# Turning narrow heads' probabilities in quarters of 32 rows, and what was rearranged to make room for it

## The chip, the cores and the metric

The kernel runs on one core of a Trainium2 chip. The metric is the device time of one execution in microseconds (us). The engines are named as in the profile: PE is TensorE's matmul stream and PEld its weight loads, DVE is VectorE, ACT ScalarE, POOL GpSimd, SP the engine that issues most DMAs. The profile also gives the clock that TensorE was granted, as a share of full speed.

## The reference, cut to what matters

Four transformer layers run one after the other over x of 16 items, 256 tokens and 128 features, in float32. Each layer is an attention part and a feed-forward part, both on a layernorm of x and both added to x. All four attentions have 16 heads; in layers 0 and 2 a head is 64 wide, in layers 1 and 3 it is 8 wide.

```python
for item in range(16):
    # layer 0: q, k normalized per head, two null keys, causal, distance bias slope[h] * -|i - j|
    # layer 1: q from a latent of 64, one k and v shared by all 16 heads of 8, causal
    # layer 2: qkv with bias, all tokens see all;   layer 3: 16 heads of 8, causal within 128 tokens
    p = softmax(q @ k.T * scale + bias_or_mask)        # per head, 256 x 256 (258 in layer 0)
    x[item] += concat_heads(p @ v) @ w_out (+ b_out)
    # feed-forward: gelu MLP (0); gated ternary MLP, two 512x512 gelu layers (1);
    # one of 8 experts per token (2); gated mix with the token before (3)
```

## The kernel before

The kernel doesn't issue its instructions in the order of its source. It describes the work as *steps*, and a planner (`Plan`, L68 to L228) decides in which order the steps of each engine are written. A step names its engine (`"AD"` is ACT or DVE, whichever is free), a rank `p`, a cost in ns, the values that it reads, writes or modifies, and, for PE, a *mode*: steps of one mode use the array in the same shape of tiles ("T" is the whole array, "S" row groups of 64, "S4" row groups of 32, "O" and "O4" column groups of 64 and 32). `Plan.run` goes through its own model of time, keeps PE in one mode while it can, and charges `SWITCH` (130 ns in its model) for a change. On the chip every engine then follows the written order, with semaphores between the engines.

Values live in *homes*, pools of equal tiles. The home "t" is the eight PSUM banks of 512 columns; a bank is taken when the first step that touches it is written and given back when the last one is. "pT" holds transposed probabilities (six tiles of 512 columns), "probs" the probabilities before that, "Q", "K" and "V" the inputs of the wide heads, "r" 512-column scratch.

**Narrow heads (layers 1 and 3, `narrow_unit`, L544).** An item has three units. A unit has sixteen blocks of 128 x 128 probabilities. Its scores are four matmul groups in row groups of 32, into four banks (mode "S4"). DVE adds the mask and takes the minimum (L563), ACT takes exponentials (L569), and then PE turns the blocks (L581): four steps in mode "T", each with four whole blocks into one bank, and each followed by a copy by ACT (L383) or DVE (L385) into one "pT" tile. The products (mode "O4", column groups of 32) need all four tiles and add up into one bank `o` per item.

**Wide heads (layers 0 and 2, `wide_unit`, L445).** An item has four units of four heads. Their blocks are turned in two halves of 64 rows (L491): the halves use two row groups of the array and two banks, in mode "S", the same as their scores.

**Layer 0 before its units (`prep0`, L716).** `project` makes q and k for the two halves of the tokens (n is 0 to 3, c is 0 or 1) and sums squares per head; POOL takes the power -1/2 (`rsqrt`, L371); `scaled` multiplies (DVE, L751), turns four whole blocks (L756, mode "T") and copies the bank into "Q" or "K". The distance bias is a table `bias` of 16 x 258 columns, one row per head, which DVE makes at the start (L676) and the reduction at L792 adds. The table shares its memory with the weights of layer 1's feed-forward, which are loaded when layer 0 is over (`to_w1`, L873).

**Layer 2 before its units (`prep2`, L1035).** The bias of v is added by DVE as v leaves PSUM (L1063), from a tile `bv` that holds it in all partitions.

**The start.** SP issues the loads of x and weights, then the load of `bv`, then two DMAs that fill the experts' row buffers with zeros (L312), in pieces of 32 elements.

Of the kernel before, what the change touches and what calls it, by code (L numbers as in the profile page):

```python
# [15 lines left out]
P = 128  # L16
# [9 lines left out]
    ("a2bq", 8), ("a2bk", 8),  # L26
# [205 lines left out]
def preln_d4_kernel(ctx: ExitStack, tc: tile.TileContext, x_in, vecs, rows, bv2, nullk, nullv,  # L232
# [50 lines left out]
    bv = cp.tile([P, 1024], F32, tag="bv", name="bv")  # L283
    nc.sync.dma_start(out=bv, in_=bv2.broadcast_to([P, 1024]))
# [22 lines left out]
    zero = cp.tile([P, D // 4], F32, tag="zero", name="zero")  # L307
    nc.gpsimd.memset(zero, 0.0)
    for part, n in enumerate(EX_BLOCKS):
        ex_rows.append(dp.tile([n * P, D], F32, tag=f"rows{part}", name=f"ex_rows{part}"))  # L310
        ex_y.append(dp.tile([n * P, D], F32, tag=f"y{part}", name=f"ex_y{part}"))
        nc.sync.dma_start(out=ex_rows[part].rearrange("(p j) (s d) -> p (j s) d", p=P, s=4),  # L312
                          in_=zero.unsqueeze(1).broadcast_to([P, 4 * n, D // 4]))
# [43 lines left out]
    plan.home("pT", many(sp, "pT", 6, [512]))  # L357
# [4 lines left out]
    plan.home("small", many(sp, "small", 5, [256]))  # L362
# [3 lines left out]
    def mm(o, lhsT, rhs, start=True, stop=True, **kw):  # L366
        nc.tensor.matmul(o, lhsT, rhs, start=start, stop=stop, **kw)  # L367

# [72 lines left out]
    def bias_x(p, name, b):  # L441
        step("POOL", p, 670, lambda e: nc.gpsimd.tensor_tensor(x_of(b), x_of(b), row_over(name, 2), ALU.add), m=[X[b]])  # L442


    def wide_unit(q, b, u, st, widths, starts, blocks, first, second, kept=None):  # L445
# [3 lines left out]
        banks, pT = [], []  # L449
# [32 lines left out]
        for pair in range(2):  # L482
            t, h = [get("t"), get("t")], [get("pT"), get("pT")]
            pT.append(h)

            def turn(e, pair=pair, t=t):
                for j in range(2):
                    for i, a in enumerate(starts):
                        for z in range(2):
                            r, c = slice(64 * z, 64 * z + 64), j * (w // 2) + i * 64  # L490
                            nc.tensor.transpose(t[z].t[:, c:c + 64], probs[pair].t[r, j, a:a + P], ident[r, r])  # L491

            step("PE", q + 8 + 2 * pair, 120 * len(starts), turn, r=[probs[pair]], w=t, mode="S")
            for z in range(2):
                evac(q + 8 + 2 * pair + z, h[z], t[z], lambda h=h, t=t, z=z: (h[z].t[:, 0:w], t[z].t[:, 0:w]), w)
        o, OT = get("t"), get("OT")

        def products(e):
            for pair in range(2):
                for k, (kc, q0, at) in enumerate(blocks):  # L500
                    for z in range(2):
                        for j in range(2):
# [5 lines left out]
                               pT[pair][z].t[:, a:a + (256 - q0) // 2].rearrange("p (c q) -> p c q", q=64),  # L508
# [3 lines left out]
        step("PE", q + 11.9, 3.36 * cols, products, r=st["V"] + pT[0] + pT[1], w=[o], mode="O")  # L512
# [31 lines left out]
    def narrow_unit(q, b, u, st, mask, mkey):  # L544
# [29 lines left out]
        pT = []  # L574
        for k in range(4):
            t, h = get("t"), get("pT")
            pT.append(h)

            def turn(e, k=k, t=t):
                for g in range(4):  # L580
                    nc.tensor.transpose(t.t[:, g * P:(g + 1) * P], probs[g // 2].t[:, g % 2, k * P:(k + 1) * P], ident)  # L581

            step("PE", q + 8 + k, 436, turn, r=probs, w=[t], mode="T")
            evac(q + 8 + k, h, t, lambda h=h, t=t: (h.t, t.t))
# [4 lines left out]
        def products(e):  # L589
# [3 lines left out]
            for k in range(4):  # L593
                hh, kc = (k, 0) if u == 0 else (2 * u - 2 + k // 2, k % 2)
                a = (256 if hh == 3 else 0) + qc * P
                for g in range(4):
                    mm(o.t[32 * g:32 * g + 32, a:a + P], st["v"](kc, g, hh), pT[k].t[:, g * P:(g + 1) * P],
                       u == 0 and k == 0, u == 2 and k == 3, skip_group_check=True)

        step("PE", q + 11.9, 900, products, r=[st["V"]] + pT, m=[o], mode="O4")  # L600
# [50 lines left out]
    bias_pool = top.enter_context(tc.tile_pool(name="a0c", bufs=1))  # L651
# [8 lines left out]
    A0, A1 = 0, first[1, 0]  # L660
    wqkv = wA[:, w0_at["qkv"]:w0_at["qkv"] + 3072]
# [4 lines left out]
    dist = bias_pool.tile([P, 258], F32, tag="dist", name="dist")  # L666
# [4 lines left out]
    bias = bias_pool.tile([P, NH, 258], F32, tag="bias", name="bias")  # L671
    slope = 2.0 ** (-2.0 ** (-(math.log2(NH) - 3.0)))

    def biases(e, u):
        for h in range(4 * u, 4 * u + 4):
            nc.vector.tensor_scalar(bias[:, h, :], dist, float(slope * slope ** h), None, ALU.mult)  # L676

    for u in range(4):
        step("DVE", 4 * u - 6, 1000, lambda e, u=u: biases(e, u), w=[f"bias{u}"])
# [23 lines left out]
    step("DVE", -13, 100, lambda e: nc.vector.tensor_scalar(nkT.rearrange("p c n -> p (c n)"), nk_ps.t[:, 0:16], kqs, None, ALU.mult),  # L703
# [12 lines left out]
    def prep0(b):  # L716
        st = {}
        lo, hi = A0 + 16 * (b - 1), A0 + 16 * b - 2
        order = ("x p00 p01 p10 p11 p20 p21 t00 p30 t01 p31 t10 v0 t11 v1 v2 t20 v3 t21 t30 t31").split()
# [11 lines left out]
        def project(n, c):  # L731
# [11 lines left out]
            if c == 1:  # L743
                step("DVE", p, 80, lambda e: nc.vector.tensor_scalar(ss[n].t, ss[n].t, 1e-24, None, ALU.max), m=[ss[n]])  # L744
                step("POOL", p - 6, 2892, lambda e: rsqrt(ss[n].t, 16), m=[ss[n]])

        def scaled(n, c):
            i, which = divmod(n, 2)
            p, raw, t = at[f"t{n}{c}"], raws[n, c], get("t")
            r = lambda: raw.t.rearrange("p (h d) -> p h d", d=64)  # L750
            step("DVE", p - 2, 598, lambda e: nc.vector.tensor_tensor(  # L751
                r(), r(), ss[n].t[:, c * 8:(c + 1) * 8].unsqueeze(2).broadcast_to([P, 8, 64]), ALU.mult), r=[ss[n]], m=[raw])

            def turn(e):
                for k in range(4):
                    nc.tensor.transpose(t.t[:, k * P:(k + 1) * P], raw.t[:, k * P:(k + 1) * P], ident)  # L756
# [730 lines left out]
```

## Time and profile before

| | |
|---|---|
| time, median of 3 runs | 2208.14 us (2207.95 to 2212.46) |
| the profiled execution | 2214.85 us |
| its span, from first to last instruction | 2213.1 us |
| mean clock granted to TensorE | 0.99 |
| matmuls and weight loads | 20879 each |
| busy: PE, PEld, DVE, ACT, POOL | 97%, 71%, 75%, 75%, 48% |

The page gives for each engine its busy time, its share of the span and its number of instructions. A busy PE includes the tail of pipelined matmuls, so that successive starts in the timeline say more about speed than durations do. Lines of the timeline give start, duration, engine, source line, operation, what is written and what is read; the shape of the weights stands as rows x columns in use. A float32 matmul appears as two instructions, a transpose as one. By the narrow and wide scores in the timeline, layer 0's units run from about 46 to 628 us, layer 1's from about 650 to 1180, layer 2's from 1158 to 1846 and layer 3's from 1837 to 2188; each layer's feed-forward runs beside the units that follow.

### The profile page before, as it was taken

What the parts mean: (1) busy time and instruction counts of PE and PEld (TensorE: products, weight loads), DVE (VectorE), ACT (ScalarE), POOL (GpSimd) and SP (SyncE); (2) the same over time, 40 slices, a digit from 0 to 9 for tenths busy, and PEclk for the clock granted to TensorE, in tenths of its full rate; (3) what the DMA queues carried; (4) which work ended last, traced back from release to release, by engine and by line L of the source; (5) the groups of instructions that cost most, each with busy time, mean ns of one, the idle gap of its engine ahead of it and who ended that gap; (6) DMA issues with size and microseconds to landing.
All of it is one profiled execution on the core that took longest, in us unless ns stands there. A gap on an engine that the chain in (4) does not pass through costs nothing.

```text
span 2213.1 us, 57690 instructions
## 1 busy us (share of the span) xinstructions
PE 2141.7 (97%) x20879; PEld 1576.0 (71%) x20879; DVE 1657.2 (75%) x6401; ACT 1669.9 (75%) x4735; POOL 1054.0 (48%) x1987
## 2 busy tenths in 40 slices
PE   6999999999999999999999999999999999998997
PEld 3767777777776566665666678888888787786775
DVE  5898888889788575666655557877766788787995
ACT  5988888989889776677756567776666577777995
POOL 6997787878851111111103235554543855226331
PEclk9999999999999999999999999999999999999998
DMA  7000000000020000000000000000432000451000
GB/s 173 2 2 2 2 2 2 2 2 2 2 92 2 1 2 1 1 1 1 1 1 1 1 1 7 7 6 3 120 111 82 26 5 19 133 164 28 12 12 11
DMA packets 58590, 57.78 MB, mean 26 GB/s; under 512 B 27824, under 2 KB 48832, under 8 KB 58304
## 3 DMA queue, kind: packets, MB, share of 16 engines
q1 hardware_dynamic: 55504, 49.06, 7.9%
q0 software_dynamic: 2048, 4.20, 0.6%
q8 instruction: 165, 2.70, 0.5%
q14 instruction: 121, 0.99, 0.1%
q10 hardware_dynamic: 752, 0.83, 0.1%
HBM read 43.85 MB, written 10.22 MB: 24 GB/s over the span
## 4 chain that ended last, share of the span: by engine, by line
PE 78%; DVE 10%; POOL 6%; ACT 3%; issue 2%; DMA 1%; another core or an unknown queue 0%; SPq 0%; POOLq 0%; ACTq 0%; DVEq 0%
PE t5x L367 9%; PE t4x L367 8%; PE t7x L367 8%; PE t2x L367 8%; PE t3x L367 7%; PE t0x L367 7%; PE t1x L367 7%; PE t6x L367 7%; PE t0x L581 1%; PE t1x L581 1%; PE t2x L581 1%; PE t3x L581 1%; PE t5x L581 1%; PE t4x L581 1%; PE t6x L581 1%
## 5 line engine op out<-in xcount | busy, mean ns | idle before, releaser
L442 POOL TENSOR_TENSOR x<-x,row_sb 128x256 f32<-128x256 f32 x48 | 35.0, 728 | 31.9 <-DVE xn1x L411 16.0
L404 POOL TENSOR_SCALAR ln_rs1x<-ln_mv1x 128x2 f32<-128x2 f32 x24 | 4.6, 193 | 76.3 <-DVE ln_mv1x L400 73.4
L991 POOL TENSOR_TENSOR x<-x,sq1x 128x512 f32<-128x512 f32 x4 | 5.1, 1280 | 73.2 <-DVE sq1x L989 73.2
L474 POOL TENSOR_SCALAR probs4x<-probs4x,sums6x 128x256 f32<-128x256 f32 (+2 forms) x40 | 17.6, 457 | 38.5 <-DVE sums6x L469 16.9
L474 POOL TENSOR_SCALAR probs2x<-probs2x,sums6x 128x256 f32<-128x256 f32 (+2 forms) x40 | 17.6, 458 | 37.4 <-DVE sums6x L469 21.5
L474 POOL TENSOR_SCALAR probs2x<-probs2x,sums2x 128x256 f32<-128x256 f32 (+2 forms) x44 | 22.2, 519 | 25.8 <-DVE sums2x L469 25.5
L404 POOL TENSOR_SCALAR ln_rs0x<-ln_mv0x 128x2 f32<-128x2 f32 x21 | 4.0, 193 | 63.2 <-DVE ln_mv0x L400 60.2
L371 POOL TENSOR_TENSOR ss0x<-ss0x,mhalf 128x16 f32<-128x16 f32 x11 | 31.9, 2902 | 2.7 <-DVE ss0x L744 2.6
L371 POOL TENSOR_TENSOR ss2x<-ss2x,mhalf 128x16 f32<-128x16 f32 x11 | 32.3, 2934 | 1.6 <-DVE ss2x L744 1.3
L404 POOL TENSOR_SCALAR ln_rs3x<-ln_mv3x 128x2 f32<-128x2 f32 x22 | 4.2, 193 | 58.2 <-DVE ln_mv3x L400 53.2
L371 POOL TENSOR_TENSOR ss1x<-ss1x,mhalf 128x16 f32<-128x16 f32 x11 | 31.9, 2898 | 0.2 <-DVE sums3x L469 0.2
L371 POOL TENSOR_TENSOR ss3x<-ss3x,mhalf 128x16 f32<-128x16 f32 x11 | 31.9, 2896 | 0.0
L474 POOL TENSOR_SCALAR probs4x<-probs4x,sums4x 128x256 f32<-128x256 f32 (+2 forms) x44 | 21.3, 499 | 21.8 <-DVE sums4x L469 21.4
L371 POOL TENSOR_TENSOR ss4x<-ss4x,mhalf 128x16 f32<-128x16 f32 x10 | 29.4, 2942 | 4.7 <-DVE ss4x L744 2.9
L404 POOL TENSOR_SCALAR ln_rs4x<-ln_mv4x 128x2 f32<-128x2 f32 x23 | 4.4, 193 | 57.1 <-DVE ln_mv4x L400 53.8
L474 POOL TENSOR_SCALAR probs4x<-probs4x,sums2x 128x256 f32<-128x256 f32 (+2 forms) x44 | 23.2, 541 | 17.1 <-DVE sums2x L469 9.3
L474 POOL TENSOR_SCALAR probs2x<-probs2x,sums0x 128x256 f32<-128x256 f32 (+2 forms) x44 | 19.4, 459 | 23.8 <-DVE sums0x L469 21.9
L371 POOL TENSOR_TENSOR ss5x<-ss5x,mhalf 128x16 f32<-128x16 f32 x10 | 29.0, 2898 | 0.0
L474 POOL TENSOR_SCALAR probs2x<-probs2x,sums4x 128x256 f32<-128x256 f32 (+2 forms) x44 | 22.1, 515 | 14.1 <-DVE sums4x L469 10.0
L991 POOL TENSOR_TENSOR x<-x,sq0x 128x512 f32<-128x512 f32 x4 | 5.1, 1280 | 45.2 <-DVE sq0x L989 45.2
L474 POOL TENSOR_SCALAR probs5x<-probs5x,sums3x 128x256 f32<-128x256 f32 (+2 forms) x44 | 20.9, 487 | 12.1 <-DVE sums3x L469 9.7
L383 ACT COPY pT1x<-t6x 128x512 f32<-128x512 f32 (+1 forms) x20 | 11.2, 560 | 19.0 <-issue 15.0
(4444 smaller groups left out, 10293.3 us busy)
## 6 DMA issues: line engine op xcount, KB each, us to landing
w0x<-in_wex_dram SPq DMA_DIRECT2D x16, 578.0 KB, 4.0
w1x<-in_wex_dram SPq DMA_DIRECT2D x15, 578.0 KB, 4.0
w2x<-in_wex_dram SPq DMA_DIRECT2D x15, 578.0 KB, 4.0
w_wA<-in_wa_dram SPq DMA_DIRECT2D x8, 512.0 KB, 6.4
ex_rows<-zero SPq DMA_DIRECT2D x2, 1472.0 KB, 23.0
x<-in_x_dram SPq DMA_DIRECT2D x8, 256.0 KB, 7.5
w_wB<-in_wb_dram SPq DMA_DIRECT2D x4, 512.0 KB, 8.0
ex_y<-bT2x SPq DMA_DIRECT2D x17, 64.0 KB, 3.4
```

The costliest lines, as they stand in the source:

```text
L367: nc.tensor.matmul(o, lhsT, rhs, start=start, stop=stop, **kw)
L371: nc.gpsimd.tensor_tensor(t, t, mhalf[:t.shape[0]].broadcast_to([t.shape[0], n]), ALU.pow)
L383: nc.scalar.copy(o, i)
L404: nc.gpsimd.tensor_scalar(ln.t[2], ln.t[1][:, :, 1], LN_EPS, 1.0, ALU.add, ALU.mult)
L442: step("POOL", p, 670, lambda e: nc.gpsimd.tensor_tensor(x_of(b), x_of(b), row_over(name, 2), ALU.add), m=[X[b]])
L474: nc.gpsimd.tensor_scalar(pr.t[:, j, a:z], pr.t[:, j, a:z], sums.t[:, i:i + 1], 1.0, ALU.mult, ALU.mult)
L581: nc.tensor.transpose(t.t[:, g * P:(g + 1) * P], probs[g // 2].t[:, g % 2, k * P:(k + 1) * P], ident)
L991: step("POOL", lo + 30, 1300, lambda e: nc.gpsimd.tensor_tensor(x, x, ys.t.rearrange("p (c d) -> p c d", d=D), ALU.add), r=[ys, "w1"], m=xx)
```

## The change

The heart is the narrow turn. A unit's sixteen blocks are turned in one step instead of four, each block in four quarters of 32 rows, quarter z into bank z, in mode "S4", so that the step takes four banks at once. The transposed probabilities of a unit lie in one tile of 4 x 512 columns, two such tiles in all, and wide units use the same tiles. The products read each block as four runs of 32 columns.

The rest rearranges what the memory for these tiles and the shape of the array touch:

- Layer 0 turns q and k in halves of 64 rows too (`turned_halves`), both halves of the tokens in one step and two banks, four steps per item instead of eight.
- The table `bias` goes. The slope moves into the reduction's factor, and k is divided by it (`steep`, `steepT`): 32 small POOL memsets at the start and one small DVE multiply for each half of k.
- Without the table, the weights of layer 1's feed-forward have a place of their own and are loaded at the start.
- The tile `bv` and its load go. The bias of v goes through the output weights once before layer 2 (`through`, and one matmul) into the output bias; v leaves PSUM by a plain copy on ACT or DVE.
- The zeros for the experts' rows come from a tile half as wide, in pieces of 16 elements, and "small" has four tiles instead of five.
- The order of `prep0`'s projections and turns is another, and layer 2's weights have a lower rank.

```diff
-    plan.home("pT", many(sp, "pT", 6, [512]))
+    plan.home("pT", many(sp, "pT", 2, [4, 512]))
-    plan.home("small", many(sp, "small", 5, [256]))
+    plan.home("small", many(sp, "small", 4, [256]))
...
+    def turned_halves(t, c, block):
+        for z in range(2):
+            r = slice(64 * z, 64 * z + 64)
+            nc.tensor.transpose(t[z].t[:, c:c + 64], block[r], ident[r, r])
...
     def narrow_unit(q, b, u, st, mask, mkey):
...
-        pT = []
-        for k in range(4):
-            t, h = get("t"), get("pT")
-            pT.append(h)
-
-            def turn(e, k=k, t=t):
-                for g in range(4):
-                    nc.tensor.transpose(t.t[:, g * P:(g + 1) * P], probs[g // 2].t[:, g % 2, k * P:(k + 1) * P], ident)
-
-            step("PE", q + 8 + k, 436, turn, r=probs, w=[t], mode="T")
-            evac(q + 8 + k, h, t, lambda h=h, t=t: (h.t, t.t))
+        pT, t = get("pT"), [get("t") for _ in range(4)]
+
+        def turn(e):
+            for k in range(4):
+                for g in range(4):
+                    for z in range(4):
+                        r, c = slice(32 * z, 32 * z + 32), 128 * k + 32 * g
+                        nc.tensor.transpose(t[z].t[:, c:c + 32], probs[g // 2].t[r, g % 2, k * P:(k + 1) * P], ident[r, r])
+
+        step("PE", q + 8, 1000, turn, r=probs, w=t, mode="S4")
+        for z in range(4):
+            evac(q + 8 + z, pT, t[z], lambda z=z: (pT.t[:, z], t[z].t))
...
-                    mm(o.t[32 * g:32 * g + 32, a:a + P], st["v"](kc, g, hh), pT[k].t[:, g * P:(g + 1) * P],
+                    mm(o.t[32 * g:32 * g + 32, a:a + P], st["v"](kc, g, hh), pT.t[:, :, 128 * k + 32 * g:128 * k + 32 * g + 32],
...
     def prep0(b):
...
+                if which == 1:
+                    step("DVE", p - 6, 80, lambda e: nc.vector.tensor_tensor(ss[n].t, ss[n].t, steep, ALU.mult), m=[ss[n]])
+
+        def scaled(which, c):
+            p, t, of = at[f"t{which}{c}"], [get("t"), get("t")], [raws[which, c], raws[2 + which, c]]
+            for i in range(2):
...
             def turn(e):
-                for k in range(4):
-                    nc.tensor.transpose(t.t[:, k * P:(k + 1) * P], raw.t[:, k * P:(k + 1) * P], ident)
+                for i in range(2):
+                    for k in range(4):
+                        turned_halves(t, i * 256 + k * 64, of[i].t[:, k * P:(k + 1) * P])
 
-            step("PE", p, 436, turn, r=[raw], w=[t], mode="T")
+            step("PE", p, 500, turn, r=of, w=t, mode="S")
...
     def first0(p, u, k, bank, pr, j, nm):
...
-                nc.vector.tensor_tensor_reduce(pr.t[:, j, a:z], bank.t[:, a:z], bias[:, 4 * u + k, 258 - (z - a):258],
-                                               -1.0, 3.0e38, ALU.add, ALU.min, nm.t[:, qc:qc + 1])
+                nc.vector.tensor_tensor_reduce(pr.t[:, j, a:z], bank.t[:, a:z], dist[:, 258 - (z - a):258],
+                                               -slopes[4 * u + k], 3.0e38, ALU.add, ALU.min, nm.t[:, qc:qc + 1])
...
-    step("SP", A1 + 8, 2000, to_w1, m=[f"bias{u}" for u in range(4)] + ["w1"], tail=20000)
+    step("SP", 8, 2000, to_w1, m=["w1"], tail=20000)
...
-    step("SP", A1 + 70, 1000, to_w2, m=["wA"], w=["w2"], tail=15000)
+    step("SP", first[0, B - 1] + 62, 1000, to_w2, m=["wA"], w=["w2"], tail=15000)
...
+    step("DVE", first[2, 0] - 12, 1800, through, r=["w2"], w=[bvo])
+    step("PE", first[2, 0] - 8, 224, lambda e: mm(bps.t[:, 0:D], ones, bvo.t[:, 0:D]), r=[bvo], w=[bps], mode="T")
+    step("DVE", first[2, 0] - 8, 200, lambda e: nc.vector.tensor_tensor(row("a2bo"), bps.t[:, 0:D], row("a2bo"), ALU.add), r=[bps], w=["a2bo"])
...
-                step("DVE", p - 8, 600, lambda e, c=c, ps=ps, V=V: nc.vector.tensor_tensor(
-                    V.t[:, c * 512:(c + 1) * 512], ps.t, bv[:, c * 512:(c + 1) * 512], ALU.add), r=[ps], w=[V])
+                evac(p, V, ps, lambda c=c, ps=ps, V=V: (V.t[:, c * 512:(c + 1) * 512], ps.t))
```

In `wide_unit` the two turns of a unit write into the one tile `pT`, at `2 * pair + z`, and the products read from there; nothing else changes in it.

## The prediction

> **What bounds the kernel now.** I read the page's busy shares and slices first, then its chain, then the busy table of one stretch in each layer, and last single rows of the timeline.
>
> ```profile
> PE 2141.7 (97%) x20879; PEld 1576.0 (71%) x20879; DVE 1657.2 (75%) x6401; ACT 1669.9 (75%) x4735; POOL 1054.0 (48%) x1987
> ...
> PE 78%; DVE 10%; POOL 6%; ACT 3%; issue 2%; DMA 1%; another core or an unknown queue 0%; SPq 0%; POOLq 0%; ACTq 0%; DVEq 0%
> ```
> TensorE is busy 97% of the span and is 78% of the chain that ended last. In the table, the columns are the stretch, its length, then busy time of PE, PEld, DVE, ACT and POOL; the rows lie in layers 0, 1, 2 and 3.
>
> ```profile
> 100.00:600.00 500.00, 497.21 (x5237) 370.29 (x5234) 429.67 (x1583) 441.15 (x1329) 407.17 (x764) 1.00 0.01 2
> 700.00:1150.00 450.00, 449.78 (x3216) 273.78 (x3215) 287.98 (x1306) 316.36 (x698) 55.86 (x74) 1.00 0.01 1
> 1200.00:1800.00 600.00, 588.01 (x6090) 477.19 (x6090) 409.51 (x1083) 395.45 (x1289) 297.92 (x606) 0.99 0.12 34
> 1850.00:2213.00 363.00, 333.21 (x3575) 256.98 (x3573) 301.92 (x1542) 287.70 (x758) 125.22 (x208) 0.96 0.20 57
> ```
> Layer 1 is TensorE alone (100%; ACT 70%, DVE 64%). Layer 0 is TensorE with ACT at 88%, DVE at 86% and POOL at 81% close behind. In layer 3 TensorE already idles (92%) and DVE has 83%, ACT 79%. So a microsecond of TensorE is worth most in layer 1, less in layer 0, little in layer 3.
>
> **The narrow turn, 48 units in layer 1 and 48 in layer 3.** The old turn, with products before it and scores behind it:
>
> ```profile
> 913.01 0.40 PE L367 MATMUL t1x<-pT1x,q3x 128*32 128x128 f32 x8
> 913.34 0.44 PE L581 MATMUL t4x<-ident,probs0x 128*128 128x128 f32 x2
> 913.62 0.38 PE L581 MATMUL t4x<-ident,probs1x 128*128 128x128 f32 x2
> 913.84 0.38 PE L581 MATMUL t5x<-ident,probs0x 128*128 128x128 f32 x2
> 914.05 0.38 PE L581 MATMUL t5x<-ident,probs1x 128*128 128x128 f32 x2
> 914.37 0.69 PE L367 MATMUL t3x<-K2x,q1x 32*128 32x512 f32 x1
> ```
> Read starts, not durations, since matmuls overlap: 0.22 us for two blocks, 0.109 us for one, 1.75 us for the sixteen of a unit. Nobody has quarters yet. The nearest row is the wide heads' turn in halves:
>
> ```profile
> 407.27 0.22 PE L491 MATMUL t4x<-ident,probs1x 64*128 64x64 f32 x1
> 407.27 0.22 PE L491 MATMUL t1x<-ident,probs1x 64*128 64x64 f32 x1
> 407.33 0.22 PE L491 MATMUL t4x<-ident,probs1x 64*128 64x64 f32 x1
> 407.33 0.22 PE L491 MATMUL t1x<-ident,probs1x 64*128 64x64 f32 x1
> ```
> Both halves of a block start together and the next block 0.062 us later (the six blocks from 407.58 on take 0.37). A half has half the moving columns, yet more than half the time, because each still loads 128 columns of weights. A quarter loads 128 columns too, so I don't expect four to take a quarter of 0.109, but 0.062 a block, if four loads run side by side as two do. The narrow scores show that they can: four loads of 32 rows start within 0.02 us and each lasts the same 0.18.
>
> ```profile
> 2002.04 0.18 PEld L367 LDWEIGHTS t3x<-K2x,q4x 32*128 32x128 f32 x1 [0.20 <-issue]
> 2002.05 0.18 PEld L367 LDWEIGHTS t5x<-K2x,q4x 32*128 32x128 f32 x1
> 2002.06 0.18 PEld L367 LDWEIGHTS t1x<-K2x,q4x 32*128 32x128 f32 x1
> 2002.06 0.18 PEld L367 LDWEIGHTS t7x<-K2x,q4x 32*128 32x128 f32 x1
> ```
> So 16 x 0.062 = 1.0 us, 0.75 less per unit: 36 us of TensorE work less in layer 1, 36 in layer 3. [...] I take 0.062, from the nearest row, and keep 0.10 as the dear end; the cheap end is 0.031 (data alone, half of the half).
>
> **Layer 0's q and k.** Eight visits of four whole blocks (0.44 us each, as 404.89 to 405.33 at L756) become four visits of eight blocks in halves: 3.5 us to 8 x 4 x 0.062 = 2.0 us an item, 24 us less over 16 items. The evacuations stay eight of 512 columns an item, at the copy's 0.59 on ACT or 0.68 on DVE; they write runs of 64 columns, priced the same, at worst 0.1 more each.
>
> **Changes of tile shape.** Each drains the array: in the rows above the last product is fed until 913.23 and the turn starts at 913.34; the first pair then takes 0.28, not 0.22. That is 0.11 + 0.06 us. By the instruction orders of the two builds, shapes change 799 times before and 886 after: 11 fewer in layer 0, 64 more in layer 1, 15 fewer in layer 2, 49 more in layer 3. At 0.16 this adds 10 us to layer 1 and 8 to layer 3 and takes 2 from each of the others.
>
> **What becomes late next.** TensorE's work falls by 26 us in layer 0, 26 in layer 1, 2 in layer 2, 28 in layer 3. Little of that reaches the end. The old turn was four steps of one bank each: the first bank was evacuated while the second was filled, beside feed-forward matmuls of the same shape. Now one step takes four of the eight banks, and four copies become ready together: two on ACT, two on DVE, about 1.3 us with the latency. Until then the unit's products (which read all four), the next scores (four banks) and the feed-forward's banks wait behind, in TensorE's fixed order. With work ready the 1.3 us are covered; with none, 48 x 1.3 = 62 us per narrow layer are exposed. In layer 1 feed-forward work mostly covers it; I charge a quarter of the units, 16 us, and 6 for other steps that queue behind: 26 - 22 = 4 us gained. In layer 3 the rest of TensorE waits for DVE's mask-and-minimum and ACT's exponentials anyway, so a lighter TensorE only idles more: of 28 us I count none, and 6 us lost to the extra shape changes that fall in the chain. In layer 0 each turn now waits for both halves' POOL powers (2.9 us each, L371), and ACT and DVE leave 12% at most: of 26 us I count 10. Sum: -10 - 4 + 6 = -8 us.
>
> **Edits costed at nothing.** The bias table's 16 DVE operations (3.5 us by 28.7 us) go, and 32 POOL memsets of about 0.1 us come ahead of the first layernorm; TensorE waits for a weight DMA until 19.45 us meanwhile, cover of 8 us. Uncovered they would cost 3. Thirty-two 16-column multiplies (0.17 each, L744's form) join DVE in layer 0, 5 us in 600, under TensorE. The value bias leaves 64 DVE adds (0.68) for copies of equal price, most still on DVE; its fold into the output bias is about 2.5 us of DVE once, before layer 2, and POOL's first bias step waits for it; a late fold would hold POOL's divisions of probabilities behind it, once, by at most those 2.5 us. SP's zero fills go to 64-byte pieces: issue 14.9 us to perhaps 30, behind all weights, and layer 1's weights queue behind them at the start, 600 us early. Layer 2's weights load earlier, off the chain. `dist` for `bias` leaves the reduction unchanged. Two big tiles for six small: a wide unit keeps one of two, not four of six; no cost.
>
> **Time.** The profiled execution took 2214.85 us, its span 2213.1. 2214.85 - 8 = 2206.9. It stands 6.7 us above the median of the three runs, 2208.14, so on their scale I predict 2200 us.
>
> **The rivals.** Partial gain, as summed, 0.52: 2192 to 2207 by how much of the four-bank wait is covered; in most of it faster by more than 0.2% (4.4 us, about what can be told from no change). The saved work comes through: layer 1's 26 and layer 0's 20 reach the end, 2162; for it the 100% of layer 1, against it the four banks; 0.06. All given back, 2208: half the units of layer 1 exposed instead of a quarter, which takes its gain and 12 more; 0.18. On the other side, issue: 64 loads and 64 matmuls in a microsecond is a rate the trace never sustains. Every nanosecond a block above 0.062 is 0.77 us in each narrow layer; layer 1's share reaches the end, so the change turns slower from about 0.072 us a block, and 0.10 costs 29 us: 2200 + 29 = 2229; 0.24.
>
> **How the numbers follow.** Faster by over 0.2%: most of the first case and the second, with a little of the third, 0.53; within: 0.16; slower: the last case with the tail of the third, 0.31. The range 2186 to 2226 leaves out the full gain, the cheap end of the quarter (2200 - 24 = 2176, which no row speaks for) and the dear end of issue.
>
> **What would show it.** Right: the quarter turn's four matmuls start together, blocks 0.062 us apart; layer 1's PE below 97% busy, with waits on DVE and ACT ahead of products and turns; layer 3 as long as before with more idle PE. Wrong: blocks 0.10 us apart, or layer 1 shorter by over 20 us, or copies into the q and k tiles above 0.8 us.

## The result, and the profile after

The changed kernel takes 2238.94 us (median of 4 runs, 2235.66 to 2241.06) where the kernel before took 2208.11 beside it: ratio 1.0133, 95% interval 1.0116 to 1.0151. It is 29 to 31 us slower. The prediction said 2200 us and a range of 2186 to 2226, so it was wrong in sign and outside its range.

The page of the changed kernel, busy shares and the slices of the granted clock, and the core's line:

```profile
PE 2135.9 (95%) x26001; PEld 1537.2 (69%) x26001; DVE 1653.0 (74%) x6418; ACT 1677.4 (75%) x4743; POOL 1055.2 (47%) x2019
...
PEclk9999999999999999999999999999999998999997
```
```profile
core 0: 2239.4 us, clock 0.972
```
TensorE is busy 6 us less than before, where the prediction took 82 us of work away, and the span is 26 us longer. The mean granted clock has fallen from 0.990 to 0.972. That looks small; over 2239 us it is (0.990 - 0.972) x 2239 = 40 us of full clock that TensorE didn't get. The table of one stretch per layer (stretch, length, busy PE, PEld, DVE, ACT, POOL, then PEclk) shows where:

```profile
100.00:600.00 500.00, 490.67 (x5742) 357.88 (x5740) 438.77 (x1634) 440.66 (x1320) 419.38 (x774) 1.00 0.01 4
700.00:1150.00 450.00, 442.94 (x4826) 254.00 (x4827) 284.07 (x1264) 304.50 (x676) 51.87 (x67) 0.98 0.01 2
1200.00:1800.00 600.00, 588.03 (x6155) 480.11 (x6152) 384.00 (x1039) 421.07 (x1335) 292.72 (x596) 0.99 0.12 34
1850.00:2239.00 389.00, 345.80 (x5975) 254.38 (x5971) 321.98 (x1593) 286.79 (x760) 128.22 (x217) 0.89 0.18 54
```
Layer 1 had clock 1.00 and now has 0.98; layer 3 had 0.96 and has 0.89. The record of the clock has two values in these two runs, full (1.00) and half (0.50), and every half stretch is a whole multiple of 3.413 us, from one to five (the last of each run ends with it). The first columns below are the time from a layer's first scores to its last; the others are the sums of half-clock stretches that begin in it (both read off the traces; layer 3's sum runs to the end). Layer 1's scores before, for example, go from 638.8 to 1145.7 us.

| | layer 0 | layer 1 | layer 2 | layer 3 | half clock: 0 | 1 | 2 | 3 | all |
|---|---|---|---|---|---|---|---|---|---|
| before | 581.5 | 507.0 | 672.2 | 337.6 | 0 | 0 | 6.8 | 37.4 | 44 |
| after | 573.3 | 519.7 | 679.3 | 362.8 | 6.8 | 20.5 | 10.2 | 88.4 | 126 |

Layer 0 is 8 us shorter, layer 1 is 13 longer and layer 3 is 25 longer. (Layer 2 is 7 longer too, but its first scores follow layer 1's last by 9 us less.) The quarters themselves run just as predicted. PE's timeline of one turn in layer 1:

```profile
1055.67 0.24 PE L585 MATMUL t6x<-ident,probs0x 32*128 32x32 f32 x1
1056.32 0.24 PE L585 MATMUL t0x<-ident,probs0x 32*128 32x32 f32 x1 [0.41 <-DVE q4x L925]
1056.33 0.24 PE L585 MATMUL t1x<-ident,probs0x 32*128 32x32 f32 x1
1056.91 0.24 PE L585 MATMUL t2x<-ident,probs0x 32*128 32x32 f32 x1 [0.34 <-DVE sq0x L960]
...
1057.00 0.22 PE L585 MATMUL t2x<-ident,probs0x 32*128 32x32 f32 x1
...
1057.06 0.22 PE L585 MATMUL t2x<-ident,probs1x 32*128 32x32 f32 x1
1057.12 0.22 PE L585 MATMUL t2x<-ident,probs1x 32*128 32x32 f32 x1
```
From 1057.00 on, bank t2 gets a block every 0.062 us. But the first block needs all four banks, and they come free one at a time: 1.24 us pass between the first quarter and the fourth, more than the 0.75 us that the turn saves. Not every turn meets this: in 32 of layer 1's 48 turns the four first quarters start within 0.05 us. Over all 48 the time from the first quarter to the fourth adds up to 12.4 us, in layer 3 to 16.0.

And then the clock. Two adjoining windows around another turn of layer 1, in the same columns, with the scores of the first window and two groups of products:

```profile
913.90:917.30 3.40, 3.01 (x71) 1.96 (x71) 3.33 (x6) 1.84 (x4) 0.00 (x0) 1.00 0.00 0
917.40:920.70 3.30, 3.30 (x35) 1.89 (x34) 3.19 (x17) 2.16 (x5) 0.00 (x0) 0.50 0.02 5
```
```profile
915.49 0.67 PE L365 MATMUL t6x<-K2x,q1x 32*128 32x512 f32 x1
915.91 0.69 PE L365 MATMUL t3x<-K2x,q1x 32*128 32x512 f32 x1
...
916.70 0.69 PE L365 MATMUL t5x<-K2x,q1x 32*128 32x512 f32 x1
916.71 0.69 PE L365 MATMUL t7x<-K2x,q1x 32*128 32x512 f32 x1
```
```profile
893.71 1.08 PE L365 MATMUL t4x<-pT0x,q3x 128*32 128x128 f32 x32
...
918.12 1.93 PE L365 MATMUL t4x<-pT0x,q3x 128*32 128x128 f32 x32
```
A window with a quarter turn and scores in it, busy 3.01 of 3.40 us, is followed by one at clock 0.50, in which a group of 32 product matmuls takes 1.93 us; the same group at full clock took 1.08. The scores in it don't start four at a time, as the loads in the prediction's rows at 2002 us do, but in ones and twos, on the banks that are free: the wait for banks thins the window as well, to 1,282 columns by the count that experiment 4 brings. In the kernel before, not one half stretch lies between the start and 1727 us.

### The profile page after: what moved, and what is told of

Read it like the earlier page. It is cut to its first block, busy times and chain, and to the rows that moved or that the text cites. A ratio compares the mean times of both kernels' runs of the same rounds, so it can differ in the third digit from the quotient of the medians.

```text
span 2239.4 us, 67931 instructions
## 1 busy us (share of the span) xinstructions
PE 2135.9 (95%) x26001; PEld 1537.2 (69%) x26001; DVE 1653.0 (74%) x6418; ACT 1677.4 (75%) x4743; POOL 1055.2 (47%) x2019
## 3 DMA queue, kind: packets, MB, share of 16 engines
q0 software_dynamic: 2048, 4.20, 0.7%
## 5 line engine op out<-in xcount | busy, mean ns | idle before, releaser
L479 POOL TENSOR_SCALAR probs0x<-probs0x,sums6x 128x256 f32<-128x256 f32 (+2 forms) x44 | 20.2, 474 | 27.9 <-DVE sums6x L474 13.6
L409 POOL TENSOR_SCALAR ln_rs2x<-ln_mv2x 128x2 f32<-128x2 f32 x22 | 4.5, 206 | 56.1 <-DVE ln_mv2x L405 55.0
L479 POOL TENSOR_SCALAR probs0x<-probs0x,sums2x 128x256 f32<-128x256 f32 (+2 forms) x40 | 20.2, 518 | 20.9 <-DVE sums2x L474 20.6
L388 ACT COPY pT1x<-t4x 128x512 f32<-128x512 f32 (+1 forms) x45 | 25.5, 567 | 3.0 <-PE t0x L585 1.5
L479 POOL TENSOR_SCALAR probs0x<-probs0x,sums4x 128x256 f32<-128x256 f32 (+2 forms) x44 | 19.6, 457 | 16.4 <-DVE sums4x L474 13.0
```

Source lines behind the costliest of these rows:

```text
L388: nc.scalar.copy(o, i)
L409: nc.gpsimd.tensor_scalar(ln.t[2], ln.t[1][:, :, 1], LN_EPS, 1.0, ALU.add, ALU.mult)
L479: nc.gpsimd.tensor_scalar(pr.t[:, j, a:z], pr.t[:, j, a:z], sums.t[:, i:i + 1], 1.0, ALU.mult, ALU.mult)
```

## The experiments

Theory A: the loss is the clock, which falls when the turn gives TensorE too little to do. (At first the author also assumed that transposes add nothing to what the clock goes by; no run shows that, and experiment 8 is against it.) Theory B: the turn takes four banks at once and waits at the head of TensorE's fixed order. Theory C: it is the rest of the change (layer 0's turns, the start). "Held order" below means that the planner is told the same costs, modes and banks, so that every engine's written order is the changed kernel's and only the matmuls inside the turn differ. Where a turn lays out its blocks another way, the products read them accordingly; the excerpts below leave that out. Differences in us are ratio minus one, times 2208, unless spans of layers are compared; those are of the profiled executions.

**1. The change without the quarters.** Narrow turn, products and pT tiles of the kernel before:

```diff
-    plan.home("pT", many(sp, "pT", 2, [4, 512]))
+    plan.home("pT", many(sp, "pT", 6, [512]))
...
-        step("PE", q + 8, 1000, turn, r=probs, w=t, mode="S4")
+            step("PE", q + 8 + k, 436, turn, r=probs, w=[t], mode="T")
```


> This is the changed kernel with the narrow turn, the products and the pT tiles of the kernel before (whole blocks, four steps of one bank, six tiles); all the rest of the change stays. [...] Theory B, the banks: the turn takes four banks at once and waits for them in TensorE's fixed order. A and B both put the loss in the quarter part: 2195 to 2212 us here, halved stretches as before, about 40 to 60 us. Theory C, the rest: the start (a halved stretch at 67 us, layer 0's first scores 3 us late) and layer 0's turns cause it: 2225 us or more here.

Measured: 2204.85 us, ratio 0.9968 (0.9954 to 0.9982), 7 us faster than before; 35 us at half clock. C falls: the rest of the change gains a little, and the quarter part loses 36 to 37 us.

**2. Idle matmuls ahead of layer 3's turns.**

```diff
         def turn(e):
+            if mkey == "mask3":
+                for i in range(1):
+                    for z in range(4):
+                        r = slice(32 * z, 32 * z + 32)
+                        mm(t[z].t[:, 256 * i:256 * i + 256], ident[r, :], mask[r, 0:256])
```


> The changed kernel in the same written order, but each of layer 3's 48 narrow turns first issues four idle matmuls into the four banks that it is about to overwrite (32 rows x 128 columns of weights, 256 moving columns each, side by side over the whole array): 0.43 us of extra TensorE work a unit, 20.6 us in all, whose results nobody uses. A, the clock: the extra matmuls count as activity, halved stretches after 1832 us fall from 88 us to under 50, and layer 3's last scores come 10 to 20 us earlier than 2205.6: 2220 to 2230 us although work was added. B, the banks: the clock is a by-product of waits, the extra work stands in front of the turn: 2240 to 2260 us.

Measured: 2257.47 us, ratio 1.0208 (1.0191 to 1.0225); clock 0.972, 127 us at half clock. It met B's number and missed A's: the extra 20.6 us of work came out as 17 us more than the changed kernel, and the half stretches didn't fall. This miss stays open. By the count that experiment 4 brings, the fill adds 512 columns to a turn, as much as experiment 5 adds, and there the half stretches did fall, to 70 us. Why the same dose ahead of the turn didn't lift the windows is not shown.

**3. Halves, two visits of two banks.**

```diff
-        step("PE", q + 8, 1000, turn, r=probs, w=t, mode="S4")
+        for half in range(2):
+            t = [get("t"), get("t")]
...
+                        turned_halves(t, 256 * (k % 2) + 64 * g, probs[g // 2].t[:, g % 2, k * P:(k + 1) * P])
+            step("PE", q + 8 + 2 * half, 500, turn, r=probs, w=t, mode="S")
```


> The changed kernel with the narrow turn in halves of 64 rows: two steps of eight blocks, two banks each, in the mode of the wide turns; a block costs the same 0.062 us, so TensorE's work saved is the same, and the planner writes another order. B, the four banks at once: most of the loss goes, 2200 to 2215 us. [...]

Measured: 2199.86 us, ratio 0.9947 (0.9930 to 0.9963): 12 us faster than before and, with experiment 11, the fastest kernel of the study, at the same price per block as the quarters, 0.062 us. Half clock 62 us. That is the good end of B's range. But halves differ from quarters in banks and in something else, as the next runs show.

**4. Whole blocks in the held order.**

```diff
-                    for z in range(4):
-                        r, c = slice(32 * z, 32 * z + 32), 128 * k + 32 * g
-                        nc.tensor.transpose(t[z].t[:, c:c + 32], probs[g // 2].t[r, g % 2, k * P:(k + 1) * P], ident[r, r])
+                    nc.tensor.transpose(t[k].t[:, g * P:(g + 1) * P], probs[g // 2].t[:, g % 2, k * P:(k + 1) * P], ident)
```


> The changed kernel in its own written order (one visit, four banks, the planner told the same cost and mode), but the sixteen blocks are turned whole, 0.109 us each instead of 0.062, 36 us more TensorE work in each narrow layer, and a change of tile shape on both sides of every turn. If the saved work is worth what the prediction took in layer 1 (all) and layer 3 (none): 2239 + 36 + some 10 for the shapes = 2285 us. [...] B, with TensorE waiting for banks and data anyway: 2245 to 2270 us.

Measured: 2228.52 us, ratio 1.0072 (1.0055 to 1.0089). What was expected is slower than the changed kernel in every case, and it is 13 us *faster*, with 72 us more TensorE work. The clock is 0.990 again:

```profile
core 0: 2229.2 us, clock 0.990
```
So in the same written order the mean clock is 0.990 with whole transposes and 0.972 with quarters. I went through the windows of 3.413 us in the traces so far and counted, for each, moving columns times the share of the array in use (rows/128 x columns/128), transposes included, a float32 matmul as the two instructions that it is, each spread evenly over its recorded duration. The windows ahead of half clock all had fewer than some 1,530 of the roughly 4,100 of the fullest windows. (The next expectation says about 1,400; this recount puts it higher.) A unit's turn is 2048 such columns in whole blocks, 1024 in halves, 512 in quarters. From here on this is A2.

**5. Halves in the held order.** The planner takes the same four banks at once; same price per block, same order, twice the columns:

```diff
-                    for z in range(4):
-                        r, c = slice(32 * z, 32 * z + 32), 128 * k + 32 * g
-                        nc.tensor.transpose(t[z].t[:, c:c + 32], probs[g // 2].t[r, g % 2, k * P:(k + 1) * P], ident[r, r])
+                    turned_halves(t[2 * (k // 2):], 256 * (k % 2) + 64 * g, probs[g // 2].t[:, g % 2, k * P:(k + 1) * P])
```


> The changed kernel in its own written order, with the same four banks taken at once and the same planner cost and mode, but each block turned in two halves of 64 rows (banks 0 and 1 for the first eight blocks, 2 and 3 for the others): the same 0.062 us a block, so the same TensorE work, order and waits. What differs is how much of the array a turn moves: weighed by the share of the array times its moving columns, a unit's whole blocks are 2048, its halves 1024, its quarters 512. Theory A2, from the halved stretches of the six traces so far: the clock halves after a window of 3.41 us with less than about 1,400 such columns, transposes included. A2: halved stretches fall from 126 us to 50 to 80 us, the granted clock rises to 0.98 or more, and the time falls by 5 to 20 us from 2239: 2219 to 2234. B, the banks and the order alone: 2237 to 2245 us, with the halved stretches as before.

Measured: 2209.33 us, ratio 0.9999 (0.9991 to 1.0007): 30 us below the quarters. Half clock 70 us, as A2 said; the gain is more than A2's 5 to 20 us, and the trace shows a second difference: with the pairs of banks one after the other, the turn needs only two banks to begin.

```profile
1041.77 0.27 PE L372 MATMUL t6x<-ident,probs0x 64*128 64x64 f32 x1
1042.42 0.27 PE L372 MATMUL t0x<-ident,probs0x 64*128 64x64 f32 x1 [0.39 <-DVE q4x L923]
1042.43 0.27 PE L372 MATMUL t6x<-ident,probs0x 64*128 64x64 f32 x1
1042.54 0.22 PE L372 MATMUL t0x<-ident,probs0x 64*128 64x64 f32 x1
```
This is the turn shown above at 1055.67. One wait of 0.39 is left; by the time that it needs the other two banks they are free.

**6. and 7. One visit or four, without quarters.** Whole blocks in the mode of whole-array steps: one visit of four banks with its true cost, and four steps of one bank into the two big tiles.

```diff
-        step("PE", q + 8, 1000, turn, r=probs, w=t, mode="S4")
+        step("PE", q + 8, 1744, turn, r=probs, w=t, mode="T")
```
and, for the other,
```diff
-        step("PE", q + 8, 1000, turn, r=probs, w=t, mode="S4")
+            step("PE", q + 8 + k, 436, turn, r=probs, w=[t], mode="T")
```


> The changed kernel with whole blocks turned in one visit that takes four banks, in the mode of whole-array steps, and the planner told its true cost (1744 ns). No quarters, no other tile shape: what is left is the one visit of four banks and the two pT tiles. B, the banks: slower than the kernel before by 5 to 20 us, 2217 to 2232 us. If only the row-group mode of the turn (the order it brings) counts and not the banks: 2200 to 2210, as the version without the quarter part.

> The changed kernel with whole blocks turned in four steps of one bank each, as before the change, but into the two big pT tiles. Tells the number of tiles from the number of banks. B, the banks: 2200 to 2212 us, as the version without the quarter part (2205). If the two tiles (a unit's products must be through before the next but one unit may be copied) cost the time: 2215 to 2235.

Measured: one visit 2229.97 us, ratio 1.0093 (1.0076 to 1.0110); four steps 2206.40 us, ratio 0.9988 (0.9981 to 0.9995). The two tiles cost nothing that shows; one visit of four banks costs 23 us in this form. In the profiled executions, which lie 30 us apart, 7 of it are in layer 1 (514.8 against 507.9) and 22 in layer 3 (356.2 against 334.4). B is real.

**8. The clock by itself.** Five stretches of 60 turns; `wait` is ACT's copy of bank 3, which every turn writes first, so that the next turn has to wait for it. The excerpt shows the third stretch.

```diff
+    Z = (3, 0, 1, 2)
+
+    def wait(n=512):
+        nc.scalar.copy(drain[0][:, 0:n], bank[3][:, 0:n])
...
+    def quarters():
+        for i in range(16):
+            for z in Z:
+                h = slice(32 * z, 32 * z + 32)
+                nc.tensor.transpose(bank[z][:, 32 * i:32 * i + 32], blk(i)[h], ident[h, h])
...
+    for n in range(60):
+        quarters()
+        wait()
```


> None of the reference is computed; x is copied to the output. Five stretches of 60 turns of 16 blocks: whole blocks, halves, quarters (in each, ACT copies 512 columns after every turn and the next turn waits for it), quarters without a wait, and four float32 matmuls of 128 columns with the wait. Estimates of the activity in a window of 3.41 us, by share of the array times moving columns, with a wait of about 1 us: whole 2500, halves 1750, quarters 870, quarters without a wait 1750, matmuls 2 x 512 in 1.4 us 2400. A2 with its bound near 1,400: full clock everywhere but in the quarters with a wait. If busy time decides: halves and quarters with a wait behave alike. If transposes don't count: the first four stretches all run at half clock and only the matmuls at full.

The table of a stretch each (PE, PEld, ACT, POOL, then PEclk); whole, halves, quarters with the wait, quarters without, matmuls:

```profile
20.00:120.00 100.00, 96.05 (x784) 84.42 (x783) 28.64 (x49) 0.00 (x0) 1.00 0.00 1
140.00:225.00 85.00, 61.37 (x1607) 54.53 (x1604) 29.28 (x50) 0.00 (x0) 1.00 0.01 2
250.00:380.00 130.00, 105.93 (x3142) 99.23 (x3139) 28.99 (x50) 0.00 (x0) 0.50 0.01 3
400.00:490.00 90.00, 88.15 (x3194) 86.68 (x3194) 0.00 (x0) 0.00 (x0) 0.50 0.02 4
500.00:550.00 50.00, 50.00 (x430) 50.00 (x429) 24.69 (x43) 0.00 (x0) 0.99 0.01 1
```
Halves leave TensorE idle for 28% of the time and keep the full clock (1.00). Quarters are busy 81% and lose it after the first window that holds nothing else (0.50). Quarters without a wait are busy 98% and don't get it back (0.50). So neither busy time nor "transposes don't count" describes the clock of these stretches; the columns by share of the array do: 2,048 a window in the halves stretch, 530 to 750 in the quarters, 840 to 1,020 without a wait.

**9. Four banks at once, without the low activity.** Experiment 5 with the pairs of banks alternating from block to block, so that all four are needed at the start and all four are done at the end, as in the quarters:

```diff
-                    turned_halves(t[2 * (k // 2):], 256 * (k % 2) + 64 * g, probs[g // 2].t[:, g % 2, k * P:(k + 1) * P])
+                    turned_halves(t[2 * (g % 2):], 128 * k + 64 * (g // 2), probs[g // 2].t[:, g % 2, k * P:(k + 1) * P])
```


> The version with halves in the changed kernel's own order, except that the pairs of banks alternate from block to block: the turn needs all four banks within its first two blocks and finishes all four at its end, as the quarters do. The activity by area stays 1024 a unit, twice that of the quarters. It splits what is left after the clock. Clock alone: 2205 to 2212 us, as with the pairs one after the other (2209). If the head-of-line wait for four banks costs something of its own (in layer 1 some 6 of the 16 us between quarters and halves lay outside halved stretches): 2214 to 2222 us.

Measured: 2221.53 us, ratio 1.0050 (1.0033 to 1.0066); half clock 78 us. B's number: 11 us over experiment 5. Its profiled execution is 5 us above the median; in it 10 us lie in layer 1 (503.4 to 513.8 us), 5 at the start and in layer 0, 1 in layer 3 (351.6 to 353.0). The quarters lie 18 us above it, with 48 us more at half clock (126 - 78), worth 24 us if TensorE is needed all through.

Since the written order is the same, the two traces can be laid side by side, one PE instruction outside the turns after the other. Then 14 us separate the two profiled executions, and they lie where one of them runs at half clock: the quarters lose 6.5 us there in layer 1 and 9.2 in layer 3. Between instructions that both ran at full clock they gain 0.5 us in layer 1 and lose 0.3 in layer 3. Laid so beside experiment 5, experiment 9 loses 7.2 us in layer 1 at full clock, and 3.2 in the two windows at half clock that it has there and experiment 5 has not.

**10. Quarters in layer 1 only**, halves as in experiment 5 in layer 3:

```diff
+            if mkey == "mask3":
+                for k in range(4):
+                    for g in range(4):
+                        turned_halves(t[2 * (k // 2):], 256 * (k % 2) + 64 * g, probs[g // 2].t[:, g % 2, k * P:(k + 1) * P])
+                return
```


> The changed kernel's order, quarters in layer 1 only and halves (pairs of banks one after the other) in layer 3. Between all quarters and all halves, layer 1 lengthened by 16 us and layer 3 by 11 to 12. If the two layers' losses are separate, as the clock theory and the bank theory both have it: 2222 to 2228 us, with no more halved stretches after 1830 us than with halves everywhere (56 us). If layer 3's loss is inherited from layer 1's lateness: 2232 us or more.

Measured: 2224.10 us, ratio 1.0062 (1.0045 to 1.0079). As expected from either theory: layer 1 is 16.5 us longer than with halves (519.9 against 503.4), layer 3 is not (351.2 against 351.6); half clock after 1830 us is 62 us, where no more than 56 were expected. The losses of the two layers are separate and add up.

**11. Smaller pT tiles for experiment 3**, four of 2 x 512:

```diff
-    plan.home("pT", many(sp, "pT", 2, [4, 512]))
+    plan.home("pT", many(sp, "pT", 4, [2, 512]))
```


> The version with halves in two steps of two banks (2200 us), with four pT tiles of 2 x 512 in place of two of 4 x 512, the same memory: a unit's first half can be copied while the unit before still holds its second. If the two big tiles hold copies back, 2 to 6 us faster: 2194 to 2198. If not, as before, 2198 to 2204, the planner's new order moving it either way.

Measured: 2200.18 us, ratio 0.9958 (0.9944 to 0.9972). The same as experiment 3; the tiles hold nothing back.

**12. The bound of the clock, from a warm start.**

```diff
+    def warm():
+        for n in range(24):
+            for z in Z:
+                nc.tensor.matmul(bank[z][:, 0:P], ident, blk(z), start=True, stop=True)
+
+    def stretch(turn, *copies):
+        warm()
+        for n in range(20):
+            turn()
+            for c in copies:
+                wait(c)
```


> None of the reference is computed; x is copied to the output. Eleven stretches of 20 turns, each after about 20 us of dense float32 matmuls, so that each starts at full clock. Estimates of activity per window (array share times columns) from the turn times of the run before: whole blocks with three, four and a half and six ACT copies after each turn 2100, 1700, 1400; halves with one and a half, two and three copies 1700, 1500, 1200; quarters with a copy of 128 columns 1340; then twice quarters without a wait (1660) and quarters with one copy (1020). Activity by area with a bound near 1,450: full clock in the first two, at the bound in the third, full in the fourth, at the bound in the fifth, halved in the sixth and seventh; quarters without a wait stay at full clock when they start there, other than in the run before, where they started halved; quarters with a copy halve. If the share of busy time decided, whole blocks with six copies (TensorE busy a third of the time) would halve far more than quarters without a wait, and halves and quarters would go alike.

Partly a miss. The dense matmuls came out mixed in among the whole turns and the first two kinds of halves, so those five stretches aren't the doses that they were meant to be. The later ones are clean (halves with three copies; quarters with a short copy; quarters without a wait):

```profile
382.00:416.00 34.00, 31.26 (x407) 29.20 (x407) 19.45 (x34) 0.00 (x0) 0.50 0.01 2
454.00:491.00 37.00, 30.58 (x1020) 28.44 (x1018) 4.24 (x16) 0.00 (x0) 0.50 0.01 4
525.00:550.00 25.00, 24.53 (x904) 24.26 (x904) 0.00 (x0) 0.00 (x0) 0.50 0.02 5
```
Halves, too, ran at 0.50 once they were spaced out: 407 matmuls of 32 such columns in 34 us are some 1,310 a window of 3.413 us. Quarters without a wait lost it even from a warm start, where I had estimated 1,660 columns: TensorE stood still for 0.95 us waiting for nothing that the profile shows, and the window had 1,159. In this run's single windows at full clock, at most 1,440 columns were followed by half clock, and 1,595 or more were not.

Over all fourteen profiled kernels, the first 25 us of each left out, there are some 7,660 windows at full clock, 159 of them followed by half clock. After more than 1,570 columns none was; after fewer than 1,380 all were. Ranked by this count, 14 windows that kept the clock lie below the highest that lost it. Ranked without the transposes it is 525. Busy time doesn't rank them at all: one window lost the clock with TensorE busy from end to end. The counts are alike on the way back: of the windows at half clock, those with over 1,560 columns were followed by full clock, those with under 1,510 by another half one.

## Why the prediction was wrong, point by point

**The narrow turn's price: right.** 0.062 us a block; the rival with 0.10 a block is refuted. It was the main case of the prediction's slower side, so that side was named for a reason that didn't happen. No run shows the 0.10 a block that this case is added up from; the runs showed 64 matmuls in 1.0 us, blocks 0.062 us apart. Whether the weight loads set that price, as the prediction has it, no run tells; halves and quarters cost the same, which fits.

**What becomes late next: the step that failed.** It charged the four-bank wait 16 us in layer 1 and 6 for the queue behind it, nothing but shape changes in layer 3, and it put the clock at nothing without a word. By layer: layer 1 -4 predicted, +13 measured; layer 3 +6 predicted, +25 measured; layer 0 -10 predicted, -8 measured. From the version with halves in two visits to the changed kernel the runs give a ladder. (That version's 2200 us is the predicted time, but by coincidence: it is another kernel.) The last two columns are the spans of the layers, first to last scores, in the profiled executions.

| step | against before, us | added | layer 1 | layer 3 |
|---|---|---|---|---|
| the kernel before | 0 | | 507.0 | 337.6 |
| halves, two visits of two banks (3) | -12 | | 503.8 | 333.8 |
| one visit in the quarters' order, pairs one after the other (5) | 0 | 12 | 503.4 | 351.6 |
| all four banks needed at once (9) | +11 | 11 | 513.8 | 353.0 |
| a quarter of the array's columns instead of half (the change) | +29 | 18 | 519.7 | 362.8 |

- The first 12 are the one visit and the order that the planner writes for it. They lie in layer 3 (18 there, less 8 after its last scores), where the prediction put the banks at nothing: whole blocks in the held order (4) are 15 us longer there than before (352.4), with no more half clock. Part of it shows in the next scores: PE is busy with scores for 79 us of layer 3 in experiment 5 and 67 in experiment 3, for 76 in one visit and 63 in four steps, as when fewer than four run at a time. That four banks gone at once cause this is argued; which wait costs how much there I didn't separate.
- The 11 are the head-of-line wait of the timeline above, 12.4 us over layer 1's turns in the changed kernel, and about 3 of them are clock that this wait costs. The prediction had the mechanism ("TensorE's fixed order") and priced only the wait behind the turn, 1.3 us for copies. It left out the wait ahead of it, since the old turn asked for one bank at a time.
- The 18 are the clock, by the closest pair of runs, 9 against the change: the same order, price and bank pattern, half the columns. What else differs, 64-row tiles beside 32-row scores, speaks for the quarters. And laid side by side, the two traces differ where the clock is halved and nowhere else in these layers (within 0.5 us). That quarters lose it by their few columns, and not by something else in them, rests on experiments 8 and 12; experiment 2 doesn't fit it yet.

**What the clock goes with: not weighed.** It isn't busy time: the window ahead of 989 us in the changed kernel was 97% busy, moved 1,512 columns and was followed by half clock. Nor do transposes add nothing to it: in experiment 8 whole blocks and halves, transposes alone, ran at 1.00 (20 to 120 and 140 to 225 us). Weighed by the share of the array, the halves move 2,048 columns a window there; the quarters, with 530 to 750, ran at 0.50 (250 to 380 us).

**A microsecond of TensorE in layer 3 is worth little: half right.** Less work there gained nothing, as said. But TensorE's slack wasn't free there. Layer 3 was already the place with half stretches before (37 of 44 us), at PEclk 0.96 in a row that the prediction shows and doesn't read. With the cheaper turn more of its windows were followed by half clock: 88 us. Of the layer's 25 us, about 10 come with the quarters; the other 15 are there with whole blocks in the held order too.

**Layer 0: right.** 8 us gained of 26, predicted 10. PE now waits up to 0.9 us ahead of q and k turns for DVE's products (L765); its longest waits ahead of those turns before were 0.3 us. The copies into the q tiles take 0.59 us on ACT and 0.68 on DVE, as before; runs of 64 columns cost nothing that shows.

**Edits costed at nothing: right as far as it shows.** The version with all of them and no quarters is 7 us faster than before. The zero fills land 43 us after issue instead of 23, beside TensorE's start. First scores come at 45.0 to 48.9 us over the experiments with this same start; that spread of a few us is one of single executions.

**What would show it.** Blocks 0.062 us apart and layer 1's PE under what it was, with waits on DVE: seen (98.4% busy, not under 97%). Layer 3 as long as before with more idle PE: not seen.

## What to carry to other kernels

When a change makes TensorE's work cheaper, count what is left in each window of 3.413 us, the step of the half stretches in these traces: moving columns times the share of the array, transposes included. In these fourteen float32 kernels, the first 25 us of each left out, half clock followed every window at full clock with fewer than 1,380 such columns and none with more than 1,570, where the fullest have some 4,100. Ask also for how many banks a step stands at the head of TensorE's order: halves in two visits of two banks had the same TensorE price as quarters in one visit of four (0.062 us a block) and were 41 us faster, some 23 of them by the banks and the order, some 18 by the clock.

## What the runs showed of the hardware

- What goes with TensorE's clock in these traces is area times columns, not time: 0.50 at 98% busy in 32-row transposes, 1.00 at 72% busy in 64-row ones. In experiment 12 windows of 3.413 us with at most 1,440 columns were followed by half clock and windows with 1,595 or more were not; over all traces it was every window with fewer than 1,380 and none with more than 1,570. The fullest windows have some 4,100.
- Quarters without a wait stayed at half clock. They move 512 columns in 1.0 us at full clock and in 1.8 us at half clock, which leaves about 970 a window (512 x 3.413 / 1.8), fewer than the 1,510 under which every window at half clock was followed by another; that stretch never came back by itself (0.50 in experiments 8 and 12). In experiment 8 denser matmuls brought it back after one window with 2,056 columns.
- Four quarter transposes in four row groups start within 0.02 us of each other, and the next four 0.062 us later: 16 ns a matmul, sustained over a turn.
- 36 us of TensorE work more or less in a layer that was 100% busy changed its length by 1.5 us (519.7 us with quarters, 518.2 with whole blocks, in one order). Side by side, the quarters gained 8.6 us of the 36 at full clock and lost 9.4 in stretches that only they ran at half clock. Part of the rest came back as scores that kept PE busy longer (81 us against 67).
